# Weight loads ahead of the image, and two norms of the lone front by one matmul with Ln and Exp

## The chip, the cores and the metric

The kernel runs on one core of a Trainium2 chip. The core has a matrix engine (PE, its weight loads shown apart as PEld), a vector engine (DVE), an activation engine (ACT, ScalarE), a general one (POOL, GpSimd), a queue for transfers (SP, SyncE) and 16 DMA engines. Each works through its own list of instructions in order and waits for the others by semaphores. The metric is device time in microseconds, as the median of several runs. Beside it there is one profiled execution, from which the durations of single instructions are taken.

## What is computed

Two layers on a batch of 8 images of 64 channels and 128 x 128 pixels, all fp32. Layer 0 is a filter whose nine weights per pixel come from a small network. Layer 1 normalises the channels, runs a two-layer, two-direction state-space scan over the 16384 pixels, and follows with convolutions and a feed-forward part. What matters for this change:

```python
# layer 0
h = conv3x3(x, w1) + b1; h = where(h >= 0, h, 0.2 * h)       # 64 -> 32 channels
w_lp = softmax(conv1x1(h, w2) + b2)                          # 9 weights per pixel
x1 = x + sum_k x_shifted[k] * (delta[k] - w_lp[k])
# layer 1, its head: the front
def layernorm(v): c = v - mean(v); return c * rsqrt(mean(c * c) + 1e-5) * w + b   # over the 64 channels
x_norm = layernorm(x1)                                       # first norm
dw = conv1x1(x_norm, dw1) ...                                # a branch, used later
seq = layernorm(x_norm)                                      # second norm
hn = seq * rsqrt(mean(seq * seq) + 1e-5)                     # third norm, of the first scan layer
# then, twice: projections, a causal convolution, softplus, and in both directions
# h[t] = exp(dt[t] * A) * h[t-1] + dt[t] * B[t] * u[t];  y = sum over 16 states of h * C
```

## The kernel before

**Preparation.** The program begins with a block that loads the weights, turns them by small matmuls against an identity (`turned`, L206), and leaves them in the form that the matmuls need. It has two halves. The first makes the weights of the convolutions (`w1n` to `parts`, L227 to L303) in three staging tiles and stores those to DRAM (L305), from where each stage loads them later (`load_weights`, L492). The second half (L320 to L375) makes the weights of the scan, for two layers with two directions each: `wx`, `wz`, `wo`, `wbc`, `wdt`, `a_neg`, `dskip`. It loads `nw`, `inx`, `inz`, `on` once for each layer and `cw`, `xdt`, `xbc`, `dtn`, `al`, `dp` for each direction, each load standing beside its use; two bias vectors per direction (L371, L372) are loaded there too.

All transfers are issued by SyncE, in the order in which they are written (fills of the padding of the `hn` rows, L387 and L388, which stand outside the block, are put in between). So ahead of the second half's loads SyncE issues the first half's loads, the clearing of the padded image in DRAM (`clear(x_img)`, L89), the copying of image 0 into it in 16 pieces (`copy_x`, L98), the tap loads (L294) and the stores of the prepared weights (L305).

**The main part** is a list of small steps. Each `plan` writes its steps to a table under a time and a phase (`at`), and the table is emitted in sorted order, so each engine's list has the order of these times. Time 0 is the first scan unit, and a scan chunk of 1024 pixels takes 16 units.

**The front** (`Front`, L497) makes the head of layer 1 for 16 chunks of an image, each of two bands of four rows (128 partitions: 64 channels of each band, 512 pixels). Chunk c of image 0 is planned at a = -199 + 24 c. Chunks 0 to 7 have the flag `alone`, as they stand ahead of the scan (L651). Successive chunks overlap by design: while chunk c has its filter applied, chunk c+1 has its `hidden` convolution and `logits`, and chunk c-1 its norms. In the order of PE's list, one step of 24 time units holds, for neighbouring chunks: `centered` (L601), the means of the first norm (L469), three parts of `hidden` (L439, L444), the spread of the first norm (L484), `pointwise` (L618), `centered` again, the means of the second norm, its spread, the means of the third, the nine `weight` matmuls (L574) and the `logits` (L527, L528).

**A norm** (`Norm`, L463) has four steps. `means`: four matmuls whose stationary operand is a quarter of the squares and whose moving operand is `half_mean` (2 columns), which puts the means of 2 x 4 row pieces on pixels as partitions. `means_out`: ScalarE adds eps and brings 128 x 8 values to SBUF (L475). `root`: POOL raises them to the power -0.5 (L478). `spread`: eight matmuls that broadcast each value over 64 channels, into a PSUM tile `rb` (L484). DVE then multiplies by `rb` (L609). An fp32 matmul shows as two records in the profile.

The accumulators in PSUM are few: one bank `acc`, one `bg`, one `mm`, each with one buffer. `hidden` and `pointwise` both use `acc`, so `pointwise` waits until `hidden_out` (L520, L521) has read it. The scan (`Chunk`, L953) has ScalarE's `decay` (L1117), DVE's scan (L1135, L1137), POOL's `drive` (L1109), products on both (L1156, L1159), and activations SiLU (L1013) and Softplus (L1041), each with a table of its own on ScalarE.

Of the kernel before, what the change touches and what calls it, by code (L numbers as in the profile page):

```python
# [8 lines left out]
F32 = mybir.dt.float32  # L9
BF16 = mybir.dt.bfloat16  # L10
AF = mybir.ActivationFunctionType
# [4 lines left out]
P = 128  # L16
C = 64
# [5 lines left out]
DI = 128  # L23
DS = 16
DTR = 4
KC = 4
DEPTH = 2
# [28 lines left out]
def kernel(ctx: ExitStack, tc: tile.TileContext, a: dict, out: bass.AP):  # L56
# [6 lines left out]
    nc = tc.nc  # L63
# [3 lines left out]
    def row(v):  # L67
        return v.rearrange("(c o) -> c o", o=1)
# [3 lines left out]
    def const(shape, name, dt=F32):  # L72
        return wp.tile(shape, dt, tag=name, name=name)
# [3 lines left out]
    def dram(shape, name):  # L77
        return dramp.tile(shape, F32, tag=name, name=name + "_dram")


    def image(name):

        return dram([C, PW * PW + PW], name)

    def pixels(img):
        return img[:, 0 : PW * PW].rearrange("c (r w) -> c r w", w=PW)

    def clear(img, lo=0, hi=PW + 1):
        nc.sync.dma_start(  # L89
            img.rearrange("c (r w) -> c r w", w=PW)[:, lo:hi],  # L90
            zero.rearrange("c (o w) -> c o w", o=1).to_broadcast([C, hi - lo, PW]),
        )
# [6 lines left out]

    zero = const([C, PW], "zero")  # L100
    nc.vector.memset(zero, 0.0)
# [11 lines left out]
    eps = const([P, 1], "eps")  # L113
# [77 lines left out]
    with tc.tile_pool(name="wspill", bufs=1) as fp, tc.tile_pool(name="wprep", bufs=2) as pp, \  # L191
            tc.tile_pool(name="wps", bufs=4, space=PSUM) as pps:
        with tc.manual_schedule():
# [51 lines left out]
            for part in ((0, 0, 0, P), (1, 0, HID, P), (2, 0, HID + P, REST_HID), (2, C, P, REST_HID)):  # L245
                _, _, r0, n = part
                fn = pp.tile([P, C], F32, tag="fn", name="fn", bufs=4)
                nc.sync.dma_start(fn[0:n, :], fw[r0 : r0 + n, :])
                fdn = pp.tile([P, 9], F32, tag="fdn", name="fdn", bufs=4)
                nc.sync.dma_start(fdn[0:n, :], fd[r0 : r0 + n, :])  # L250
                parts.append((part, fn, fdn))
            clear(x_img)
            for i in range(NCH):
                copy_x(0, i)
# [63 lines left out]
                )  # L318

            for l in range(DEPTH):  # L320
                nw = pp.tile([P, 1], F32, tag="nw", name="nw")
                for h in range(2):
                    nc.sync.dma_start(nw[h * C : (h + 1) * C, :], row(a["L1_conv_m_norm_w"][l]))
                inx = pp.tile([DI, C], F32, tag="inx", name="inx")
                nc.sync.dma_start(inx, a["L1_conv_in_proj_w"][l, 0:DI, :])
                inz = pp.tile([DI, C], F32, tag="inz", name="inz")
                nc.sync.dma_start(inz, a["L1_conv_in_proj_w"][l, DI : 2 * DI, :])
# [3 lines left out]
                on = pp.tile([C, DI], F32, tag="on", name="on")  # L331
                nc.sync.dma_start(on, a["L1_conv_outproj_w"][l])
                for g in range(2):
                    to_blocks(
                        wo[:, l, g].rearrange("p i c -> p (i c)"),
                        turned(twice(on[:, C * g : C * g + C], C, C)[:, 0, :], ident[0:C, 0:C], P, C), C, C,
                    )
                for d in range(2):
                    cw = pp.tile([DI, KC], F32, tag="cw", name="cw")
                    nc.sync.dma_start(cw, a["L1_conv_conv_w"][l, d])  # L340
# [6 lines left out]
                    xdt = pp.tile([DTR, DI], F32, tag="xdt", name="xdt")  # L347
                    nc.sync.dma_start(xdt, a["L1_conv_xproj_w"][l, d, 0:DTR, :])
                    xbc = pp.tile([2 * DS, DI], F32, tag="xbc", name="xbc")
                    nc.sync.dma_start(xbc, a["L1_conv_xproj_w"][l, d, DTR : DTR + 2 * DS, :])  # L350
                    t = turned(xbc, ident[0:32, 0:32], DI, 32)
                    nc.scalar.copy(wbc[:, l, d, :], t[:, 0:32])
                    dtn = pp.tile([DI, DTR], F32, tag="dtn", name="dtn")
                    nc.sync.dma_start(dtn, a["L1_conv_dtproj_w"][l, d])
# [3 lines left out]
                    al = pp.tile([DI, DS], F32, tag="al", name="al")  # L358
                    nc.sync.dma_start(al, a["L1_conv_A_log"][l, d])
# [12 lines left out]
                    nc.sync.dma_start(dtb[:, l, d : d + 1], row(a["L1_conv_dtproj_b"][l, d]))  # L372
                    dp = pp.tile([DI, 1], F32, tag="dp", name="dp")
                    nc.sync.dma_start(dp, row(a["L1_conv_Dp"][l, d]))
                    nc.vector.tensor_scalar(dskip[:, l, d, :], ident, dp, None, ALU.mult)  # L375


# [18 lines left out]
    def at(time, phase, fn, *args):  # L396
        steps.setdefault((time, phase), []).append((fn, args))
# [65 lines left out]
    class Norm:  # L463


        def means(self, ps, sq):
            self.mp = ps("ms")
            for w in range(ROWS):
                nc.tensor.matmul(  # L469
                    self.mp[:, 2 * w : 2 * w + 2], sq[:, W * w : W * w + W], half_mean, start=True, stop=True  # L470
                )

        def means_out(self):
            self.r = wk.tile([P, 2 * ROWS], F32, tag="r", name="r", bufs=4)
            nc.scalar.activation(self.r, self.mp[:, 0 : 2 * ROWS], AF.Identity, bias=eps)  # L475

        def root(self):
            nc.gpsimd.tensor_tensor(self.r, self.r, neg_half, ALU.pow)  # L478

        def spread(self, ps):  # L480
            self.rb = ps("rb")
            for w in range(ROWS):
                for h in range(2):
                    nc.tensor.matmul(  # L484
                        self.rb[C * h : C * h + C, W * w : W * w + W],
                        self.r[:, 2 * w + h : 2 * w + h + 1].to_broadcast([P, C]), ident, start=True, stop=True,
                    )
# [9 lines left out]
    class Front:  # L497
# [860 lines left out]
```

## Time and profile before

| | |
|---|---|
| median of 3 runs | 29446.01 us (29431.68 to 29453.83) |
| the profiled execution | 29481.41 us, span 29479.5 us |
| granted PE clock, mean | 0.864 |
| busy share of the span | PE 79%, PEld 25%, DVE 93%, ACT 63%, POOL 94% |
| POOL's first `drive` | 505.0 us after the span's start |
| last of the preparation (`dskip`, L375) | 146.61 us |
| exponentials L539 of chunks 1 to 7 | 203.04, 243.68, 285.73, 326.54, 367.42, 408.34, 449.28 us |

The span runs from the first instruction to the last. Times of single instructions are microseconds from the span's start. A line of a timeline is one group of like instructions: start, length, engine, line of the source, operation, output and inputs, shapes, count, and in brackets how long the engine stood idle before it and what ended that.

### The profile page before, as it was taken

Reading aid. Unit: us, or ns where it says so; the run is one execution under the profiler, and the core shown is the slowest. Engines: PE = TensorE matmul, PEld = TensorE weight load, DVE = VectorE, ACT = ScalarE, POOL = GpSimd, SP = SyncE. Lnnn points to the kernel's source line nnn. Section 1 sums busy time; section 2 is a strip of 40 time slices with the busy share of each in tenths; the row PEclk is TensorE's granted clock in tenths of the full one; section 3 lists DMA queues with packets and bytes.
Section 4 is the critical chain, followed back from the end, with each engine's and each line's share of the span. In section 5 each row is a group of like instructions: output and inputs, shape, how many; then the busy total and the mean of one; then the engine's idle time right before and its main releaser. Section 6 shows DMA issues by size and latency. Waiting matters only on the chain. (4 is left out here: it accounts for less than half of the span.)

```text
span 29479.5 us, 312296 instructions
## 1 busy us (share of the span) xinstructions
PE 23358.6 (79%) x97708; PEld 7341.1 (25%) x97708; DVE 27316.3 (93%) x17567; ACT 18561.4 (63%) x28361; POOL 27648.1 (94%) x8732
## 2 busy tenths in 40 slices
PE   6666888878788787887878778787787877878678
PEld 3211222223222232222322223222222222222123
DVE  4999999999999999999999999999999999999997
ACT  3666666666666666666666666666666666666663
POOL 3999999999999999999999999999999999999994
PEclk7777888988889888988888888898888988889789
DMA  5776777767777678776787767777677776777674
GB/s 121 225 244 215 229 249 242 235 216 234 252 234 236 218 230 255 236 232 216 238 251 235 231 220 236 252 238 230 220 241 248 239 224 222 243 245 238 217 249 142
DMA packets 2592280, 6762.81 MB, mean 229 GB/s; under 512 B 431270, under 2 KB 736822, under 8 KB 2589462
## 3 DMA queue, kind: packets, MB, share of 16 engines
q1 hardware_dynamic: 2590614, 6742.83, 71.4%
q8 instruction: 773, 12.66, 0.2%
q14 instruction: 893, 7.32, 0.1%
HBM read 5509.49 MB, written 1265.19 MB: 230 GB/s over the span
## 5 line engine op out<-in xcount | busy, mean ns | idle before, releaser
L1109 POOL TENSOR_TENSOR bu<-dup,bp 128x2048 f32<-128x2048 f32 x4096 | 18564.5, 4537 | 370.7 <-DVE w L1137 238.3
L1117 ACT ACTIVATE w<-dtp,a_neg 128x1024 f32<-128x1024 f32 x8192 | 9159.6, 1118 | 800.4 <-DVE hs L1135 341.3
L1156 POOL TENSOR_TENSOR hs<-hs,cp 128x1024 f32<-128x1024 f32 x2832 | 6678.4, 2358 | 250.2 <-ACT state L1149 191.9
L1159 DVE TENSOR_TENSOR hs<-w,cp 128x1024 f32<-128x1024 f32 x5360 | 6562.7, 1224 | 361.7 <-DMA cp<-bc_dram 132.8
L1137 DVE TENSOR_TENSOR_SCAN w<-w,state,bu 128x1024 f32<-128x1024 f32 x2683 | 6290.4, 2345 | 292.8 <-ACT w L1117 291.9
L1135 DVE TENSOR_TENSOR_SCAN w<-w,state,bu 128x1024 f32<-128x1024 f32 x2677 | 6278.7, 2345 | 243.6 <-ACT w L1117 241.3
L1175 PE MATMUL y<-hs,sel_y 128*32 128x512 f32 x32768 | 5121.8, 700 | 60.6 <-POOL hs L1156 60.3
L1149 ACT COPY state<-w 128x1 f32<-128x1 f32 x5360 | 837.9, 156 | 5524.7 <-DVE hs L1159 5474.4
L1137 DVE TENSOR_TENSOR_SCAN hs<-w,state,bu 128x1024 f32<-128x1024 f32 x1413 | 3308.2, 2341 | 209.9 <-issue 121.7
L1135 DVE TENSOR_TENSOR_SCAN hs<-w,state,bu 128x1024 f32<-128x1024 f32 x1419 | 3321.0, 2340 | 41.3 <-ACT state L1149 16.7
L1168 PE MATMUL y<-xc,dskip 128*64 128x512 f32 x4096 | 1577.5, 860 | 1660.6 <-ACT yv L1192 1392.1
L987 PE MATMUL xp<-hn,wx 128*128 128x512 f32 x4096 | 2350.5, 703 | 669.3 <-ACT xc L993 469.2
L819 PE MATMUL fp<-fw,bgw 128*128 128x512 f32 (+1 forms) x5760 | 2270.0, 637 | 104.6 <-ACT ga L866 71.7
L1149 ACT COPY state<-hs 128x1 f32<-128x1 f32 x2832 | 541.4, 191 | 1968.6 <-DVE hs L1137 1018.6
L1175 PEld LDWEIGHTS y<-hs,sel_y 128*32 128x32 f32 x32768 | 729.8, 117 | 3676.1 <-issue 2444.1
L1028 PE MATMUL dp<-xc,wdt 128*128 128x512 f32 x2048 | 1237.5, 688 | 462.1 <-ACT dt L1035 362.6
L478 POOL TENSOR_TENSOR r<-r,neg_half 128x8 f32<-128x8 f32 x768 | 1262.6, 1644 | 300.7 <-ACT r L475 279.2
L1117 ACT ACT_TABLE_LOAD x1134 | 1454.9, 1283 | 20.0
L1065 POOL TENSOR_TENSOR dt<-dt,xc 128x1024 f32<-128x1024 f32 x512 | 1211.2, 2366 | 221.8 <-DMA dt_dram<-dt 187.7
L825 PE MATMUL fp<-fw,bgw 64*128 64x512 f32 (+1 forms) x5760 | 1415.3, 610 | 0.0
L589 PE MATMUL acc<-t,ident 128*128 128x512 f32 x2160 | 1265.5, 669 | 85.6 <-DVE hc L609 84.7
L987 PEld LDWEIGHTS xp<-hn,wx 128*128 128x128 f32 x4096 | 830.8, 216 | 1988.2 <-issue 964.3
(214 smaller groups left out, 25747.8 us busy)
## 6 DMA issues: line engine op xcount, KB each, us to landing
bp<-bc_dram SPq DMA_DIRECT2D x4096, 256.0 KB, 4.2
dup<-du_dram SPq DMA_DIRECT2D x4096, 256.0 KB, 5.0
dtp<-dt_dram SPq DMA_DIRECT2D x4096, 256.0 KB, 5.0
cp<-bc_dram SPq DMA_DIRECT2D x4096, 256.0 KB, 5.0
hn<-hn_dram SPq DMA_DIRECT2D x1024, 256.5 KB, 4.9
dt_dram<-dt SPq DMA_DIRECT2D x512, 512.0 KB, 3.4
du_dram<-dt SPq DMA_DIRECT2D x512, 512.0 KB, 2.6
yf_dram<-yv SPq DMA_DIRECT2D x512, 256.0 KB, 4.7
```

The source lines that it names most:

```text
L819: nc.tensor.matmul(o, wpair[:, i, g, m], self.win[h][:, i : i + ROWS, 0:W], start=(i == 0), stop=False)
L825: nc.tensor.matmul(o, wlast[rows, i, g, m], self.win[h][rows, i : i + ROWS, lo : W + lo], start=False, stop=(i == 2),)
L987: nc.tensor.matmul(self.xp[h], wx[:, self.l, self.d, i, :], self.hn2[:, s.start + 2 * i : s.stop + 2 * i], start=(i == 0), stop=(i == 1),)
L1109: nc.gpsimd.tensor_tensor(bu, self.dup[self.pairs[k][1]], self.over_pair("bp", k), ALU.mult)
L1117: nc.scalar.activation(w, self.dtp[gp][:, i, :], AF.Exp, scale=a_neg[:, self.l, self.d, g, j : j + 1])
L1135: nc.vector.tensor_tensor_scan(to, w, bu, s0, ALU.mult, ALU.add)
L1137: nc.vector.tensor_tensor_scan(to[:, ::-1], w[:, ::-1], bu[:, ::-1], s0, ALU.mult, ALU.add)
L1149: nc.scalar.copy(self.column(u), h[:, T - 1 : T] if self.d == 0 else h[:, 0:1])
L1156: nc.gpsimd.tensor_tensor(hs, hs, c, ALU.mult)
L1159: nc.vector.tensor_tensor(hs, w, c, ALU.mult)
L1168: nc.tensor.matmul(self.y[C * h : C * h + C, :], dskip[:, self.l, self.d, C * gp : C * gp + C], self.xc[:, s], start=True, stop=False,)
L1175: nc.tensor.matmul(self.y[lo : lo + 32, :], sel_y, hs[:, i, s], start=False, stop=(k % 4 == 3))
```

## The change

It has two parts.

*Loads.* The 34 loads of the second half of the preparation (`nw` to `dp`, all but the bias vectors) are issued in a loop of their own ahead of `clear(x_img)` and `copy_x`. Their tiles get as many buffers as there are layers, or layers and directions, and are looked up in the dictionary `own` where they are used. What is computed from them, and where, stays.

*Norms.* For chunks with `alone`, norms `n1` and `n2` (not `n3`) use one matmul with a 128 x 128 constant `mean_c`, which has 1/64 in its two diagonal blocks, so that the mean over the 64 channels arrives on every channel. ScalarE takes the logarithm of mean plus eps in place in PSUM, then the exponential of -0.5 times that. `root` and `spread` do nothing for these. Ahead of the list of steps, ScalarE is told to load a table set that holds both functions.

```diff
+EXP_AND_LN = "natural_log_exp_and_others"
...
+    mean_c = const([P, P], "mean_c")
+    nc.vector.memset(mean_c, 0.0)
+    nc.vector.memset(mean_c[0:C, 0:C], 1.0 / C)
+    nc.vector.memset(mean_c[C:P, C:P], 1.0 / C)
...
+            own = {}
+            for l in range(DEPTH):
+                nw = pp.tile([P, 1], F32, tag="nw", name="nw", bufs=2)
+                for h in range(2):
+                    nc.sync.dma_start(nw[h * C : (h + 1) * C, :], row(a["L1_conv_m_norm_w"][l]))
+                own[l, "nw"] = nw
+                inx = pp.tile([DI, C], F32, tag="inx", name="inx", bufs=2)
+                nc.sync.dma_start(inx, a["L1_conv_in_proj_w"][l, 0:DI, :])
+                own[l, "inx"] = inx
...
+                for d in range(2):
+                    cw = pp.tile([DI, KC], F32, tag="cw", name="cw", bufs=4)
+                    nc.sync.dma_start(cw, a["L1_conv_conv_w"][l, d])
+                    own[l, d, "cw"] = cw
...
             clear(x_img)
             for i in range(NCH):
                 copy_x(0, i)
...
-                inx = pp.tile([DI, C], F32, tag="inx", name="inx")
-                nc.sync.dma_start(inx, a["L1_conv_in_proj_w"][l, 0:DI, :])
...
+                inx = own[l, "inx"]
...
     class Norm:
+        alone = False
+
         def means(self, ps, sq):
+            if self.alone:
+                self.rb = ps("rb")
+                nc.tensor.matmul(self.rb, mean_c, sq, start=True, stop=True)
+                return
             self.mp = ps("ms")
...
         def means_out(self):
+            if self.alone:
+                nc.scalar.activation(self.rb, self.rb, AF.Ln, bias=eps)
+                nc.scalar.activation(self.rb, self.rb, AF.Exp, scale=-0.5)
+                return
...
         def root(self):
+            if self.alone:
+                return
...
         def spread(self, ps):
+            if self.alone:
+                return
...
-            self.alone = a + FRONT_STEP < -2
+            self.alone = n1.alone = n2.alone = a + FRONT_STEP < -2
...
     with tc.manual_schedule():
+        nc.scalar.preload_act_table_set(EXP_AND_LN)
         for key in sorted(steps):
```

More of the change, by code (lines that the diff above doesn't have):

```diff
@@ L251 @@
                 parts.append((part, fn, fdn))
+            own = {}
[7 more added lines that the diff above has]
+                own[l, "inx"] = inx
+                inz = pp.tile([DI, C], F32, tag="inz", name="inz", bufs=2)
+                nc.sync.dma_start(inz, a["L1_conv_in_proj_w"][l, DI : 2 * DI, :])
+                own[l, "inz"] = inz
+                on = pp.tile([C, DI], F32, tag="on", name="on", bufs=2)
+                nc.sync.dma_start(on, a["L1_conv_outproj_w"][l])
+                own[l, "on"] = on
+                for d in range(2):
+                    cw = pp.tile([DI, KC], F32, tag="cw", name="cw", bufs=4)
+                    nc.sync.dma_start(cw, a["L1_conv_conv_w"][l, d])
+                    own[l, d, "cw"] = cw
+                    xdt = pp.tile([DTR, DI], F32, tag="xdt", name="xdt", bufs=4)
+                    nc.sync.dma_start(xdt, a["L1_conv_xproj_w"][l, d, 0:DTR, :])
+                    own[l, d, "xdt"] = xdt
+                    xbc = pp.tile([2 * DS, DI], F32, tag="xbc", name="xbc", bufs=4)
+                    nc.sync.dma_start(xbc, a["L1_conv_xproj_w"][l, d, DTR : DTR + 2 * DS, :])
+                    own[l, d, "xbc"] = xbc
+                    dtn = pp.tile([DI, DTR], F32, tag="dtn", name="dtn", bufs=4)
+                    nc.sync.dma_start(dtn, a["L1_conv_dtproj_w"][l, d])
+                    own[l, d, "dtn"] = dtn
+                    al = pp.tile([DI, DS], F32, tag="al", name="al", bufs=4)
+                    nc.sync.dma_start(al, a["L1_conv_A_log"][l, d])
+                    own[l, d, "al"] = al
+                    dp = pp.tile([DI, 1], F32, tag="dp", name="dp", bufs=4)
+                    nc.sync.dma_start(dp, row(a["L1_conv_Dp"][l, d]))
+                    own[l, d, "dp"] = dp
             clear(x_img)
@@ L320 @@
             for l in range(DEPTH):
-                nw = pp.tile([P, 1], F32, tag="nw", name="nw")
-                for h in range(2):
-                    nc.sync.dma_start(nw[h * C : (h + 1) * C, :], row(a["L1_conv_m_norm_w"][l]))
-                inx = pp.tile([DI, C], F32, tag="inx", name="inx")
-                nc.sync.dma_start(inx, a["L1_conv_in_proj_w"][l, 0:DI, :])
-                inz = pp.tile([DI, C], F32, tag="inz", name="inz")
-                nc.sync.dma_start(inz, a["L1_conv_in_proj_w"][l, DI : 2 * DI, :])
+                nw = own[l, "nw"]
+                inx = own[l, "inx"]
+                inz = own[l, "inz"]
                 inx2 = twice(inx, DI, C)[:, 0, :]
@@ L330 @@
                 nc.vector.tensor_scalar(wz[:, l, :], t[:, 0:DI], nw, None, ALU.mult)
-                on = pp.tile([C, DI], F32, tag="on", name="on")
-                nc.sync.dma_start(on, a["L1_conv_outproj_w"][l])
+                on = own[l, "on"]
                 for g in range(2):
@@ L338 @@
                 for d in range(2):
-                    cw = pp.tile([DI, KC], F32, tag="cw", name="cw")
-                    nc.sync.dma_start(cw, a["L1_conv_conv_w"][l, d])
+                    cw = own[l, d, "cw"]
                     taps = by_taps(inx2, cw, DI, KC)
@@ L346 @@
                         nc.vector.tensor_scalar(wx[lo, l, d, at // 2, :], t[lo, 0:DI], nw[lo], None, ALU.mult)
[L347 to L350, printed above, removed]
+                    xdt = own[l, d, "xdt"]
+                    xbc = own[l, d, "xbc"]
                     t = turned(xbc, ident[0:32, 0:32], DI, 32)
                     nc.scalar.copy(wbc[:, l, d, :], t[:, 0:32])
[L353 to L354 removed]
+                    dtn = own[l, d, "dtn"]
                     dtt = pp.tile([DTR, DI], F32, tag="dtt", name="dtt")
@@ L357 @@
                     nc.scalar.copy(wdt[:, l, d, :], turned(xdt, dtt, DI, DI)[:, 0:DI])
-                    al = pp.tile([DI, DS], F32, tag="al", name="al")
-                    nc.sync.dma_start(al, a["L1_conv_A_log"][l, d])
+                    al = own[l, d, "al"]
                     nc.scalar.activation(al, al, AF.Exp)
@@ L372 @@
                     nc.sync.dma_start(dtb[:, l, d : d + 1], row(a["L1_conv_dtproj_b"][l, d]))
-                    dp = pp.tile([DI, 1], F32, tag="dp", name="dp")
-                    nc.sync.dma_start(dp, row(a["L1_conv_Dp"][l, d]))
+                    dp = own[l, d, "dp"]
                     nc.vector.tensor_scalar(dskip[:, l, d, :], ident, dp, None, ALU.mult)
```

## The prediction

> **What bounds the kernel now.** I read the page first: its slices are level at 9 tenths on DVE and POOL from the second slice on, and lower in the first. The change touches the weight preparation and the front of image 0 only, so the first slice is what counts. Next I read windows of 50 us over the first 600 us.
>
> ```profile
> 50.00:100.00 50.00, 4.04 (x18) 3.91 (x18) 3.31 (x13) 0.58 (x3) 0.00 (x0) 0.50 1.14 104
> 300.00:350.00 50.00, 35.60 (x148) 18.98 (x148) 14.04 (x25) 11.94 (x25) 6.35 (x7) 0.66 0.19 51
> 550.00:600.00 50.00, 42.08 (x187) 13.07 (x186) 48.58 (x36) 31.08 (x49) 48.64 (x17) 0.86 0.63 207
> ```
>
> The columns are the window, its length, then PE, PEld, DVE, ACT, POOL busy, granted clock, DMA share, GB/s. There are three regimes: at 50 us only the DMAs work; at 300 us the front runs alone and no engine is full, so a chain of dependent steps sets the pace; from about 505 us the scan fills POOL, then DVE. Time lost ahead of the scan is added to the end one for one, as every engine works its list in the written order. Then the waits of the first 520 us, and SyncE's own waits:
>
> ```profile
> ACT twice L203 <- DMA inx<-in_L_conv_in_proj_w: 51.1, 1, 51.1
> SPq L431 <- DVE dskip L375: 18.2, 1, 18.2
> ```
>
> The second half of the preparation (the scan's weights) waits 51.1 us for its first load; then the first window load (L431) waits 18.2 us for the last instruction of that preparation, whose SBUF it takes over. The timeline of SyncE's queue shows why:
>
> ```profile
> 22.88 0.59 SPq L89 DMA_DIRECT2D x_dram<-zero  x1
> 88.27 4.68 SPq L294 DMA_DIRECT2D w<-in_L_conv_ffn_dw_w  x4
> 100.77 0.32 SPq L305 DMA_DIRECT2D w_dram<-w  x1
> 103.52 0.73 SPq L325 DMA_DIRECT2D inx<-in_L_conv_in_proj_w  x1
> 147.03 2.38 SPq L431 DMA_DIRECT2D xa<-x_dram  x4
> ```
>
> The image is cleared (issued at 22.88) and copied (the queue shows the sixteen copies from 55.38 to 88.27), and inx stands behind both. Preparation then runs from 106.5 to 146.9, that is 40.4 us. Last, the timeline of one front step, 40.88 us from one L539 (326.54) to the next (367.42):
>
> ```profile
> 332.54 1.64 POOL L478 TENSOR_TENSOR r<-r,neg_half 128x8 f32<-128x8 f32 x1 [2.26 <-ACT r L475]
> 337.97 1.09 PE L484 MATMUL rb<-ident,r 128*64 128x128 f32 x16
> 342.07 1.12 PE L618 MATMUL dwp<-hc,bgw 128*128 128x512 f32 x2 [3.00 <-ACT ha L521]
> 343.97 2.08 PE L601 MATMUL cp<-hc,center 128*128 128x512 f32 x2 [0.78 <-ACT dwt L622]
> 347.21 1.87 PE L469 MATMUL ms<-half_mean,sq 128*128 128x2 f32 x8 [0.61 <-ACT hc L606]
> 349.46 1.64 POOL L478 TENSOR_TENSOR r<-r,neg_half 128x8 f32<-128x8 f32 x1 [14.33 <-ACT r L475]
> 351.15 1.98 PE L484 MATMUL rb<-ident,r 128*64 128x128 f32 x16 [1.62 <-POOL r L478]
> 353.24 0.69 DVE L609 TENSOR_TENSOR hc<-hc,rb 128x512 f32<-128x512 f32 x1 [2.99 <-PE rb L484]
> ```
>
> The first norm's spread (337.97) stands on PE behind the hidden convolution; the second norm is a bare chain from 347.21 to 353.24.
>
> [...] mean granted clock is 0.66 in the front, and L601 takes 2.08 us here but 1.13 at 471.75. [...] L622 (bias) 687 ns, L605 (square) 597 ns. [...] here a load takes 1283 and the next activation follows at once (475.42, then 476.71).
>
> **The change, part by part.**
>
> *A. Loads moved.* 34 DMAs of the scan's weights (nw two per layer, inx, inz, on, and six per direction) leave the place behind L305 and go ahead of the image clear. In that place layer 0 took 11.5 us (101.14 to 112.68), 1.9 of it for the four bias loads that stay; layer 1's unblocked issues come to about 7.5. I take 16 us of SyncE (15 to 17). So clear, copies, wtap loads and weight stores all come 16 us later: the clear at 38.9, the last store at 116.8. What still stands before the first window load is eight bias loads of 0.47 (3.8) and a zero fill (0.5): about 121.5 in place of 147.03. Preparation, its weights landed by about 41, starts at 56.2, ends near 97, and is hidden behind the image with 24 us to spare. What is late next is the image, on SyncE's queue. Gain 25.5; I take 25. If that cover were gone (image late by 25), A would be nothing. The clear of dw_img (DMA share over 1 from 150 to 190) and the first xb wait on it simply shift along.
>
> *B. Norms one and two, chunks 0 to 7 (n3 keeps its old form).* Per norm, out go 8 small matmuls, one 0.27 Identity, one POOL power (1.64), 16 spread matmuls; in come one 128x128x512 fp32 matmul (2 records, priced by L601), Ln (0.69) and Exp (0.60).
>
> n1: the mean matmul takes the place of L469's 1.05 at full clock, so hidden starts as before (332.08). Ln, Exp, the L609 multiply and L613 end near 335.1, all under hidden, which ends at 337.97. ScalarE's hidden_out needs only PE: start 338.1, so L618 at 339.4 in place of 342.07: 2.67 less.
>
> n2: at half clock, 2.11 (L601's start to L605's) + 0.73 + 0.65 = 3.49 from start to L609, in place of 6.03: 2.54 less. After L609 the step is as before: DVE's multiplies and PE's logits are unchanged.
>
> That is 5.21 for each of the six steps from 203.0 to 449.3: 31.3.
>
> *Clock.* With dwp 2.7 us nearer to hidden, the idle stretch that now drops the clock at 343.7 mostly disappears; [...] I estimate that 4 steps in 5 keep full clock through L601 and the mean (0.9 us each, from 2.08 against 1.13), less 0.25 for a later warm-up now and then: 1.2 a step, 7.2 in all. The bounds are -5 (hidden caught cold for a window, each step) and +11. I take +5.
>
> *Chunk 6* (449 to 502) has chunk 0's first convolution and SiLU between. Hidden_out then waits for L993, so n1 gives 1.0; the convolution that ran at half clock (467.04, 3.36 us against 1.98) may give 1.4; Ln and Exp put SiLU's table load back by 1.1. Between 0 and 5; I take 2.5.
>
> *Chunk 7* runs with the scan's start: POOL loses two powers (3.3 us) while full, but the tables of SiLU, Softplus and Exp alternate, so Ln and Exp need 2 to 4 extra loads of 1.28, some of them ahead of a decay that has 2.3 us of slack. Between -3 and +4; I take 1.
>
> *Costed at nothing:* the preload of the table (1.28, ScalarE idle from 144 to 162 before and waiting for the image after), three memsets on DVE at 2 us (about 0.1 to 0.2 each, L109 to L111; DVE idles 8.3 us before w1n lands), more SBUF.
>
> Sum: 25 + 31.3 + 5 + 2.5 + 1 = 65 us. The profiled execution took 29481.41 us with a span of 29479.5, so 2 us lie around it, outside the change; its steps are priced in that execution, and I take the sum from the median, which stands 35 us below it: 29446 - 65 = 29381.
>
> **The rivals.**
> 1. *The image is later than I count* (more descriptors in flight, window loads waiting for the 1.3 MB store): A falls to 12, total 52, 29394. For: DMA share is over 1.2 while it moves. Against: stores landed in 4 to 6 us.
> 2. *Ln and Exp do not share a table*, so every norm pays two loads: n2's 2.54 is eaten by 2.57, n1's stays hidden, and the clock gains nothing; 25 + 16 + 1 = 42, 29404. Against: the preload names the set.
> 3. *Hidden falls to half clock*: 11.3 us in place of 5.9, B gives nothing, 25 remains, 29421. Against: cp and the mean keep PE busy ahead of it.
> 4. *Slower: the scan itself is changed for good.* The new constant and the pools move SBUF addresses; 512 scan chunks of some 56.6 us each (28,970 us behind the start) outweigh the start if each takes over 65/512 = 0.127 us more. At 0.25 it gives 29446 - 65 + 128 = 29509. For: POOL and DVE are over 90% busy together. Against: L1109 stays between 4484 and 4660 ns over all its buffers, and the order is the same.
>
> **How the numbers follow.** Forecast 0.70, with its own range 29368 to 29398; rivals 0.12, 0.07, 0.05, 0.06. Range 29360 to 29415: it takes in rivals 1 and 2 and the forecast's unknowns, and leaves out 3 and 4. A measurement of this kernel can't tell less than 0.2% from no change, that is 59 us, 29387. The forecast lies just past it: three quarters of its chance (0.53) with a little of rival 1 fall beyond, together 0.55; within 0.40 (the rest of the forecast, rivals 1 to 3); slower 0.05 (rival 4).
>
> **What would show it.** A: no 51 us wait on inx; first L431 near 121.5 and not released by dskip. B: six steps of about 35 us between L539s in place of 41; L618 right behind L521; no L478 for n1 and n2 before 500 us. Clock: L601 at 1.1 behind L618. Scan rows unchanged to the nanosecond or so. The prediction is wrong if L431 comes after 130, if table loads appear between the steps, or if L1109, L1137, L1159 have other means.

## The result

The kernel after takes 29376.54 us (median of 15 executions, 29346.33 to 29416.47), the kernel before on the same chip 29439.03 (29417.36 to 29453.83): 62.5 us less, a ratio of 0.9981 with a 95% interval of 0.9974 to 0.9988. The profiled execution of after took 29416.47 us, with a span of 29414.7. Both profiled executions are long ones: that of before (29481.41 us) lies above its 15 timed ones, that of after is the longest of its 15.

The windows of the kernel after at the three places shown for the one before (columns: window, length, busy time of PE, PEld, DVE, ACT, POOL, granted clock, DMA share, GB/s):

```profile
50.00:100.00 50.00, 31.46 (x118) 25.48 (x118) 20.04 (x83) 6.26 (x31) 0.00 (x0) 0.50 1.14 122
300.00:350.00 50.00, 39.19 (x131) 18.71 (x132) 19.80 (x37) 13.57 (x28) 3.41 (x7) 0.64 0.23 64
550.00:600.00 50.00, 41.93 (x171) 15.01 (x167) 46.45 (x37) 27.92 (x44) 48.13 (x16) 0.81 0.59 196
```

At 50 us PE now works (31.46 us, before 4.04) while the DMAs carry the image: that is the second half of the preparation. At 300 us the front still runs alone, a little denser. The scan's window looks as before. SyncE's queue in the timeline of the kernel after:

```profile
23.98 0.59 SPq L265 DMA_DIRECT2D inx<-in_L_conv_in_proj_w  x1
39.31 0.59 SPq L91 DMA_DIRECT2D x_dram<-zero  x1
69.04 29.95 SPq L100 DMA_DIRECT2D x_dram<-in_x  x16
99.09 3.83 SPq L334 DMA_DIRECT2D w<-in_L_conv_ffn_dw_w  x4
111.14 0.32 SPq L345 DMA_DIRECT2D w_dram<-w  x1
117.31 2.40 SPq L460 DMA_DIRECT2D xa<-x_dram  x4
```

inx goes out at 23.98 instead of 103.52, and its wait of 51.1 us is gone. The clear goes out 16.4 us later (39.31 against 22.88). The last instruction of the preparation (`dskip`, now L404) is done at 96.5, 21 us ahead of the first window load, which comes at 117.31 instead of 147.03. So it is now the image, and the stores behind it, that hold up the first window load. One front step of the kernel after, 33.57 us from the exponential at 272.38 to the next at 305.95:

```profile
276.72 1.12 PE L500 MATMUL rb<-sq,mean_c 128*128 128x512 f32 x2 [0.69 <-ACT sq L648]
282.68 1.05 PE L473 MATMUL hp<-xa,bgw 64*32 64x512 f32 x4
285.11 1.12 PE L661 MATMUL dwp<-hc,bgw 128*128 128x512 f32 x2 [1.38 <-ACT ha L564]
287.01 1.12 PE L644 MATMUL cp<-hc,center 128*128 128x512 f32 x2 [0.78 <-ACT dwt L665]
289.30 1.12 PE L500 MATMUL rb<-sq,mean_c 128*128 128x512 f32 x2 [0.83 <-ACT hc L649]
290.47 0.66 ACT L510 ACTIVATE rb<-rb,eps 128x512 f32<-128x512 f32 x1 [0.75 <-PE rb L500]
291.16 0.58 ACT L511 ACTIVATE rb<-rb 128x512 f32<-128x512 f32 x1
291.78 0.69 DVE L652 TENSOR_TENSOR hc<-hc,rb 128x512 f32<-128x512 f32 x1 [0.40 <-ACT rb L511]
```

Nothing stands between hidden's last matmul (282.68) and dwp (285.11) but `hidden_out`. The second norm goes from the start of cp (287.01) to its multiply (291.78) in 4.77 us; before it took 9.27 (343.97 to 353.24). And cp and the mean behind it run at full clock, 1.12 each, where cp took 2.08 before.

The instructions of the scan take as long as before: drive 4539 ns in the mean (before 4537), the larger group of scans 2345 (2345), DVE's product 1225 (1224).

To follow the 73.4 us by which the first scan starts earlier (440.79 against 514.23), each front step can be cut at four points that all kernels have: the exponential of the softmax, dwp (the output of `pointwise`), the second cp (the output of the second `centered`) and the issue of the next window load (xa). The first norm lies in the first stretch, the second in the third. The table gives the mean over the six steps between the exponentials of chunks 1 and 7, in us, with the time of the first window load and the start of the first scan.

| kernel | first xa | exponential to dwp (n1) | dwp to 2nd cp | 2nd cp to xa issue (n2) | to the next exponential | step | first scan |
|---|---|---|---|---|---|---|---|
| before | 147.03 | 15.57 | 2.06 | 11.16 | 12.24 | 41.04 | 514.23 |
| after | 117.31 | 13.31 | 1.90 | 7.23 | 12.25 | 34.70 | 440.79 |
| loads alone | 120.62 | 15.72 | 2.06 | 11.21 | 12.25 | 41.24 | 486.06 |
| norms alone | 143.98 | 13.42 | 1.90 | 7.30 | 12.24 | 34.86 | 473.86 |
| n1 alone, with loads | 122.04 | 13.67 | 1.90 | 9.76 | 12.24 | 37.58 | 464.99 |
| n2 alone, with loads | 121.52 | 17.10 | 1.90 | 8.59 | 12.26 | 39.85 | 480.61 |
| no preload | 120.57 | 14.49 | 1.90 | 8.54 | 12.24 | 37.18 | 468.42 |
| dummy matmuls | 121.61 | 14.45 | 1.90 | 6.70 | 13.99 | 37.04 | 469.58 |
| chunk 7 in the old form | 121.34 | 13.22 | 1.90 | 7.09 | 12.25 | 34.46 | 445.24 |
| the same, and n3 | 116.39 | 12.61 | 1.90 | 7.23 | 12.43 | 34.17 | 436.13 |
| n3, chunk 7 new | 116.78 | 12.51 | 1.90 | 7.12 | 12.45 | 33.98 | 435.18 |
| after, again | 125.76 | 13.44 | 1.90 | 7.15 | 12.26 | 34.76 | 452.97 |

The two stretches that hold no norm keep their length to 0.2 us, apart from the kernel with dummies. All that the change does in a step is in the two stretches named n1 and n2.

### The profile page after: what moved, and what is told of

Read it like the earlier page. It is cut to its first block, busy times and chain, and to the rows that moved or that the text cites. A ratio compares the mean times of both kernels' runs of the same rounds, so it can differ in the third digit from the quotient of the medians.

```text
span 29414.7 us, 311582 instructions
## 1 busy us (share of the span) xinstructions
PE 23404.7 (80%) x97356; PEld 7317.8 (25%) x97356; DVE 27321.0 (93%) x17570; ACT 18581.3 (63%) x28381; POOL 27624.7 (94%) x8716
## 5 line engine op out<-in xcount | busy, mean ns | idle before, releaser
L1152 POOL TENSOR_TENSOR bu<-dup,bp 128x2048 f32<-128x2048 f32 x4096 | 18571.6, 4539 | 369.3 <-DVE w L1180 236.3
L1202 DVE TENSOR_TENSOR hs<-w,cp 128x1024 f32<-128x1024 f32 x5360 | 6563.9, 1225 | 322.5 <-DMA cp<-bc_dram 91.5
L1180 DVE TENSOR_TENSOR_SCAN w<-w,state,bu 128x1024 f32<-128x1024 f32 x2683 | 6292.2, 2345 | 297.7 <-ACT w L1160 296.7
L1180 DVE TENSOR_TENSOR_SCAN hs<-w,state,bu 128x1024 f32<-128x1024 f32 x1413 | 3308.6, 2342 | 227.5 <-issue 121.5
```

The source lines that it names most:

```text
L1152: nc.gpsimd.tensor_tensor(bu, self.dup[self.pairs[k][1]], self.over_pair("bp", k), ALU.mult)
L1180: nc.vector.tensor_tensor_scan(to[:, ::-1], w[:, ::-1], bu[:, ::-1], s0, ALU.mult, ALU.add)
L1202: nc.vector.tensor_tensor(hs, w, c, ALU.mult)
```

## Experiments

**Each part alone.** Loads alone: the kernel after with the old norms and without the preload.

```diff
-            self.alone = n1.alone = n2.alone = a + FRONT_STEP < -2
+            self.alone = a + FRONT_STEP < -2
...
-        nc.scalar.preload_act_table_set(EXP_AND_LN)
```

> The moved loads alone, with the old norms. Theory (the parts add up, each only shifts what stands behind it): first window load at 117 us in place of 147, first L539-like exponential near 136.5 (30 less), chunk 0's step some 3 us shorter as in the changed kernel, every later front step 41 us as before, POOL's first drive near 472 (33 less than 505.0); time 27 to 37 us less. Rival (the parts share their gain, the earlier image being worth little without the shorter steps): drive less than 20 us earlier, time within 20 of before.

Norms alone: the kernel before with the new `Norm`, its constant, its flags and the preload; the loads stay behind the image.

> The new norms alone, with the loads where they were. Theory: first window load at 147.0 as before; six front steps of 33.5 to 35 us in place of 41, drive near 466 (38 to 40 less than 505.0), chunk 0 of the scan 1 to 3 us longer for the table loads of chunk 7; time 30 to 42 us less. Rival (it is the clock's phase, which the moved loads set): steps of 36 to 38, the second centered matmul at 2.1 us in some of them.

Loads alone took 29431.51 us against 29452.1 for before, a ratio of 0.9994 (0.9985 to 1.0002): 20.6 us, which the interval does not tell from nothing. In its trace the first window load is 26.4 us earlier, the scan 28.2, and the steps are those of before. That is less than was expected (33 at the first drive, 27 to 37 at the end), but the rival's sign, a drive less than 20 us earlier, did not come. Norms alone took 29422.47, a ratio of 0.9990 (0.9983 to 0.9996), 29.6 us less; so a tenth of a per cent could be told from nothing here, half of what the prediction allowed for. Its steps are 34.86 in the mean, with one of six second cps at half clock, and the scan starts 40.4 us earlier, though its first load is only 3.0 earlier. At the start of the scan the parts add up to 28.2 + 40.4 = 68.6, and both together gave 73.4. Of the 4.8 between them, 3.1 is chunk 6's step, 55.79 with the norms alone and 52.73 in the kernel after: in it n1's stretch is 2.6 us longer, with hidden at half clock.

**Each norm alone.**

```diff
-            self.alone = n1.alone = n2.alone = a + FRONT_STEP < -2
+            self.alone = n1.alone = a + FRONT_STEP < -2
```

> The changed kernel with only the first norm in the new form for the lone chunks. Theory (the first norm's gain is 2.67 us a step, and it is what brings the pointwise matmul close enough to the hidden convolution for the clock to stay full, so the clock's gain comes with it): second centered matmul at 0.70 us a record in most steps, steps of 36.5 to 37.5 us. Rival (the two are independent, the clock's gain comes with the denser mean matmuls): records at 1.22, steps of 38.2.

and with `n2.alone` in the place of `n1.alone`:

> The changed kernel with only the second norm in the new form. Theory: the second centered matmul stays at half clock (1.22 us a record) in all or nearly all steps, as the idle stretch after the hidden convolution is as long as before; steps of 38.2 to 38.6 us (40.9 less 2.54). Rival: records at 0.70 and steps of 36.5 to 37.5.

In one execution each they took 29411.74 and 29438.92 us, with 29454.09 for before. n1 alone shortens its own stretch by 1.90, and also that of n2, which it does not touch, by 1.40: dwp follows hidden sooner, and the second cp (1.12 in all six steps) keeps the full clock. n2 alone shortens its own stretch by 2.57, at half clock throughout, and n1's becomes 1.53 longer. A timeline of one such step shows where:

```profile
217.55 1.86 PE L504 MATMUL ms<-half_mean,sq 128*128 128x2 f32 x8 [0.69 <-ACT sq L648]
219.34 1.92 PE L468 MATMUL hp<-xa,bgw 128*32 128x512 f32 x4
221.19 1.67 PE L473 MATMUL hp<-xa,bgw 64*32 64x512 f32 x4
```

The mean of n1 takes 1.86 (before 1.05 at 248.46), hidden's first two groups 1.92 and 1.67 (before 1.05 each). The windows of the same trace, PE alone (window, length, PE busy, granted clock, DMA share, GB/s), show the clock rise:

```profile
215.65:219.07 3.42, 2.73 (x10) 0.50 0.56 135
219.07:222.48 3.41, 3.41 (x10) 0.50 0.23 63
222.48:225.89 3.41, 3.41 (x16) 1.00 0.00 0
```

The full clock comes at 222.48, 9.7 us behind the exponential; in the step of before that starts at 243.68 it comes at 248.14, 4.5 us behind. So the 2.57 gained on n2 is nearly all paid back in n1's stretch in four steps of six (40.7 to 40.8 each; the other two 37.9 and 38.1). The expectation had cp right, at half clock, and the steps wrong in these four (38.2 to 38.6). For n1 alone it held nearly, with 37.58 for 36.5 to 37.5. The two singles give 3.46 + 1.19 = 4.65 a step, both together 6.34. The difference lies in n1's stretch, which the pair shortens by 2.26 and the singles, added up, by 0.37, and there it is hidden's clock.

**The table set.** The preload is taken away.

```diff
-        nc.scalar.preload_act_table_set(EXP_AND_LN)
```

> The changed kernel without the preload of the table set. Theory (Ln and Exp sit in one set only because it is loaded by name): two table loads of 1.28 in each of the 14 norms of chunks 0 to 6, those of the first norm hidden under the convolution, those of the second on the path: steps of about 37.3 in place of 34.7, drive 15 to 18 us later than in the changed kernel. Rival (the set is chosen so without being told, or the loads are hidden): steps of 34.7, drive at 432.

29432.42 us in one execution. ScalarE's list in the timeline of one second norm:

```profile
303.87 1.28 ACT L510 ACT_TABLE_LOAD   x1
305.17 0.66 ACT L510 ACTIVATE rb<-rb,eps 128x512 f32<-128x512 f32 x1
305.85 1.28 ACT L511 ACT_TABLE_LOAD   x1
307.14 0.58 ACT L511 ACTIVATE rb<-rb 128x512 f32<-128x512 f32 x1
```

Without the preload a load of 1.28 us stands ahead of the logarithm (303.87) and another ahead of the exponential (305.85), and so in each of these norms: 48 loads in the first 600 us in place of 20. A step is 2.48 longer than in the kernel after, 1.31 of it in n2's stretch and 1.18 in n1's, where the mean and hidden's first group meet the half clock (2.08 and 1.84 in the step from 284.34). The scan starts 27.6 us later: 3.3 of that is the first window load, 14.9 the six steps, and 8.0 chunk 6's step (60.73 against 52.73), where two groups of the scan's first convolution also run at half clock (3.48 and 3.78 instead of 1.88 and 1.98). The expectation had the steps right (37.3; measured 37.18) and the first drive too early (15 to 18 us later; measured 27.1). In the kernel after no load stands between the preload (0.72) and SiLU's (402.27), while 14 norms take their logarithm and their exponential in between; no row of before had shown that the named set serves both. It takes the explicit load to get this here.

**Where the loads stand.** The moved loads go behind the clear instead of ahead of it, still ahead of the copies.

```diff
+            clear(x_img)
             own = {}
             for l in range(DEPTH):
...
-            clear(x_img)
             for i in range(NCH):
                 copy_x(0, i)
```

> The changed kernel with the clearing of the image issued ahead of the moved loads, so that SyncE issues these while the clearing runs. Theory (the image's chain sets the front's start, and 16 us of SyncE's issuing stand in it, of which part would be hidden behind the clearing): first window load at 108 to 114 us in place of 117 to 121. Rival (the transfers are full from the clearing on, so it makes no difference where the issue time is, or the loads then stand behind the clearing's descriptors and the preparation becomes the wait): 117 or later.

The rival held; 29440.64 us in one execution, with 29454.09 for before. SyncE's queue in the timeline of this kernel:

```profile
22.90 0.59 SPq L91 DMA_DIRECT2D x_dram<-zero  x1
23.53 24.54 SPq L263 DMA_DIRECT2D nw<-in_L_conv_m_norm_w  x2
...
66.34 31.42 SPq L100 DMA_DIRECT2D x_dram<-in_x  x16
...
120.39 2.39 SPq L460 DMA_DIRECT2D xa<-x_dram  x4
```

The two small loads right behind the clear take 24.54 us to issue. In the kernel after it is a fill of `hn_dram` that stands there and takes 23.13 (39.95 to 63.08). In the kernel before, the same fill takes 24.18 (23.51 to 47.69). So the queue stood still for 23 to 25 us behind the clear with the fill next as with the loads next, and the issues of the loads are not hidden in it: the copies start at 66.34 instead of 69.04. Those 2.7 us are given back by four fills of `hn_dram`, which stood behind the clear and are now issued right ahead of the first window load (117.72 to 120.2). The first window load comes at 120.39, and the place ahead of the clear is as good as this one.

**Chunk 7.** Chunks 0 to 6 in the new form, chunk 7, whose norms run beside the first scan chunk, in the old.

```diff
-            self.alone = n1.alone = n2.alone = a + FRONT_STEP < -2
+            self.alone = a + FRONT_STEP < -2
+            n1.alone = n2.alone = self.alone and self.c < 7
```

> The changed kernel with the new norms for chunks 0 to 6 only, chunk 7 keeping the old ones, so that the four table loads at the scan's start are gone and two powers are back on POOL. Theory (those loads cost what chunk 0 of the scan lost): first scan 1 to 2 us sooner behind the first drive than the 8.4 of the changed kernel or the same, chunk 0 near 59.7 in place of 61.1. Rival (the loss is the transfers' issue on SyncE, which the tables do not touch): chunk 0 stays at 61 or more, with DVE's wait for cp of about 2.4 us still there.

29408.06 us in one execution. In the kernel after, the timeline of ScalarE shows what chunk 7 pays:

```profile
431.76 1.28 ACT L510 ACT_TABLE_LOAD   x1
...
433.74 1.28 ACT L511 ACT_TABLE_LOAD   x1
```

and the same pair again at 459.79 and 461.76. The preload helps here only until another set is loaded (SiLU's at 402.27): behind it Ln and Exp of chunk 7 pay one load of 1.28 us each, four in all, as in the kernel without the preload (459.39 and 461.36, 486.47 and 488.45 there). Without the four loads the first scan chunk lasts 57.70 us, with them 61.11; before it lasted 59.70. So the expectation (59.7) had the cause right for this one chunk. By chunk 12 no gain can be seen: from the last exponential ahead of the scan to the first scan of chunk 12 it is 699.2 us here and 699.7 in the kernel after, but 695.8 in the repeat of the kernel after below and 695.4 before.

**A clock held up on purpose.** If clock is what is lost, a busier PE might keep it: two dummy matmuls beside each of the `weight` matmuls and one beside each piece of the logits, into a PSUM tile that nobody reads.

```diff
+    def warm(n):
+        y = py.tile([P, N], F32, tag="y", name="warm")
+        for _ in range(n):
+            nc.tensor.matmul(y, identb[0:65, :], wts[0], start=True, stop=True)
...
                 nc.tensor.matmul(o, self.ha[0:64, W * r : W * r + W], w2a, start=False, stop=True)
+                if self.alone and 0 < self.c:
+                    warm(1)
...
             nc.tensor.matmul(self.wb, sel_k[:, k].rearrange("k h c -> k (h c)"), self.wt, start=True, stop=True)
+            if self.alone and self.c < 7:
+                warm(2)
```

> The changed kernel with idle matmuls added in the lone front (two bf16 ones of 512 columns behind each filter-weight matmul, one behind each row of the logits), whose output nobody reads, to keep PE's activity up in the half step that runs at half clock. Theory (clock is what is left in the step): logits, third norm's spread and first centered matmul run at full clock, steps 31.5 to 33.5 us in place of 34.7, drive 8 to 20 us sooner. Rival (the added matmuls cost PE what the clock gives, or the clock does not respond to them): steps of 34.5 to 36.

The rival's mechanism held, at steps of 35.0 to 37.5, mostly above its range of 34.5 to 36; 29431.12 us in one execution. The timeline of PE, and one window of it:

```profile
275.97 0.60 PE L495 MATMUL warm<-wt,identb 65*128 65x512 bf16 x2
...
276.79 1.06 PE L495 MATMUL warm<-wt,identb 65*128 65x512 bf16 x2
...
279.84:283.25 3.41, 3.41 (x10) 0.50 0.00 0
...
290.55 2.08 PE L653 MATMUL cp<-t,center 128*128 128x512 f32 x2
```

The clock falls in the midst of the dummies (a pair takes 0.60, then 1.06) and stays low to the next cp, although PE has no gap worth naming from 276.40 to 288. The dummies cost 1.74 us between xa and the next exponential; n2's stretch is now 6.70 in every step, but n1's is 14.45.

Which windows at half clock are followed by full clock can be counted in all 14 profiles of this case together. Between 200 and 400 us their granted clock changes only on a grid of 3.41 us. There they hold 512 windows of this grid at half clock, and 78 of them are followed by full clock. If the logits (fp32 with 18 columns) and all bf16 matmuls (the dummies and the `weight` matmuls among them) are left out, the remaining matmuls leave PE idle for at most 0.45 us in each of the 78, and for at least 0.49 us in each of the other 434. (The ends of matmuls are modelled in a profile, so the border is no exact figure.) If all matmuls are counted there is no such border: 48 windows without idle time, 18 of them in this kernel, are not followed by full clock. Why there is a border only without these matmuls, for their type or for their shape, no run held apart. n2 alone agrees with it: the window from 215.65 above is idle for 0.69 us and half clock goes on, the next is filled and full clock follows. So does the one step of the kernel after that meets hidden at half clock: the window from 272.05 is idle for 0.44 us and the clock rises, the one from 340.32 for 0.51 us and it does not.

**The third norm too.** Chunks 0 to 5 take n3 by the same matmul; chunk 7 stays in the old form.

```diff
-            self.alone = n1.alone = n2.alone = a + FRONT_STEP < -2
+            self.alone = a + FRONT_STEP < -2
+            n1.alone = n2.alone = self.alone and self.c < 7
...
-            at(a + 38, REST, lambda: n3.means(bg_tile, self.sq))
+            n3.alone = self.alone and self.c < 6
+            at(a + 38, REST, lambda: n3.means(mm_tile if n3.alone else bg_tile, self.sq))
```

> Chunks 0 to 6 take n1 and n2 by one matmul, chunks 0 to 5 also n3; the rest takes the power, and everything else is as in the kernel after. Theory (what a norm costs on this path is its spread matmul and its way through the power, so n3 gives up its spread ahead of the first cp as well): no L527 behind the exponential, the first cp starts at the exponential instead of 2.02 us behind it, steps of 31.5 to 33.5 us in place of 33.6 to 37.1, first drive at 188 to 199 (208.17 in the kernel after), chunk 0 near 57.7 instead of 61.1, median 9 to 18 us under the kernel after, 29359 to 29368 on the chip and beside the before of the kernel after, ratio to before 0.9975 or less. Rival 1 (the clock takes it back: with less work ahead of the first cp the full clock comes later in the step, as with n2 alone, where n1's stretch grew from 13.5 to 16.0): steps stay at 34.5 to 36, first drive at 204 to 209, ratio 0.998. Rival 2 (a gain at the front no longer reaches the end): the first drive comes early, yet the ratio stays at 0.998 or above.

The expectation has a slip: 208.17 is the sum of the six steps of the kernel after, not the time of its first drive (432.38), and "188 to 199" was meant for that sum. Measured: the sum is 205.03, the first drive 426.92, the median 29375.05 us against 29415.26 for before on that chip, a ratio of 0.9983 (0.9976 to 0.9990). The mechanism of rival 1 held, at steps of 33.4 to 34.5, a little below its range. The spread is gone and cp starts beside the exponential, but the timeline shows what it meets:

```profile
269.38 2.07 PE L644 MATMUL cp<-t,center 128*128 128x512 f32 x2
272.14 2.07 PE L500 MATMUL rb<-sq,mean_c 128*128 128x512 f32 x2 [0.69 <-ACT sq L648]
274.14 1.92 PE L468 MATMUL hp<-xa,bgw 128*32 128x512 f32 x4
275.99 1.38 PE L473 MATMUL hp<-xa,bgw 64*32 64x512 f32 x4
```

cp, mean and hidden's first two groups run at half clock, 2.07, 2.07, 1.92 and 1.38, where the kernel after had 1.64, 1.12, 1.05 and 1.05 in the step from 272.38. In the kernel after the spread of n3 and cp fill the window from 272.05 but for 0.44 us, and the clock rises 3.1 us behind the exponential. Without the spread the window with cp and the mean is idle for 0.69 us, and the clock rises 6.6 us behind. Of the 2.02 us taken out ahead of cp, 0.61 is left in n1's stretch (13.22 to 12.61), and n3's mean gives 0.18 of that back (12.25 to 12.43). It doesn't measurably beat the kernel after. Rival 2 is not ruled out either: the drive came 5.5 us earlier than in the kernel after, yet the ratio stayed above 0.998.

> As the kernel after (n1 and n2 in the new form for chunks 0 to 7), with n3 also in that form for chunks 0 to 5. Beside the run of the kernel with chunk 7 left in the old form it tells whether n3 and chunk 7 add up. Theory: steps as in that run, 31.5 to 33.5; chunk 0 stays near 61.1, since chunk 7's norms still pay four loads of tables beside the scan; so 2 to 4 us more than the other run. Rival (the clock takes it back): steps 34.5 to 36.

With chunk 7 in the new form as well: steps of 33.3 to 34.6, three of them at the lower end of the rival's range (34.5 to 36) and three at the upper end of the theory's (31.5 to 33.5), the first scan chunk 60.49, and 29323.88 us in its one execution, 91 us below before. It was run again, with the kernel after beside it on one chip.

> The kernel after, unchanged, beside the kernel with n3 in the new form and beside runs of before on the same chip. Theory (the front's gain, 68 to 73 us at the start of the scan, reaches the end whole): 60 to 73 us below before, ratio 0.9975 to 0.998. Rival (the scan gives a part back): 30 to 50 us below, ratio 0.9983 to 0.999, as the run of the six chunks with n3 had it (0.9983, 40 us).

> n1 and n2 in the new form for chunks 0 to 7, n3 for chunks 0 to 5, timed. In its one look it took 29323.88, 91 us below before, though its scan started only 5.6 us ahead of the kernel after and chunk 12 9 us ahead. Theory (that look caught the good end of a wander which the scan has in any kernel): median 3 to 12 us below the kernel after on the same chip, the profile at the start of the scan again near 435. Rival (with this front the scan falls into a better pattern for good): 25 to 60 us below the kernel after.

The kernel after took 29424.63 us (29403.68 to 29461.08), 51.7 below the 29476.37 of before there, a ratio of 0.9982 (0.9973 to 0.9991), between the two expectations and near its first value of 0.9981. The one with n3 took 29422.25, 54.1 below, a ratio of 0.9981 (0.9972 to 0.9991): 2.4 us below the kernel after, so the 91 us of one execution did not come again, and the theory's 3 to 12 us were just missed. Its scan started at 447.91 and not near 435: the first window load came 8.2 us later than in the run before (124.96), and the step from chunk 0's exponential to chunk 1's took 4.3 us more.

## Why the prediction was right

It said 29381 us from a gain of 65. Measured were 62.5 and, on another chip, 51.7, both with intervals that hold 65 (some 35 to 77 and 27 to 80 us). At the start of the scan, where the terms can be told apart, the gain is 73.4 and 61.3 in the two profiles of the kernel after. The mechanism was right in its main parts. That the median came within 2.5 us of the sum is in part luck: in the profile the terms miss by up to 5 us each, up and down, and a part of the gain at the start is not found in the medians.

*A, 25 us: right.* The first window load is 29.7 us earlier in one profile and 21.3 in the other; in all profiles with moved loads it stands between 116.39 and 125.76, with a median of 121.0, against the 121.5 worked out. What moves it is when the copies of the image can start behind the clear (69.04 in the first profile, 72.22 in the second) and how long they take (29.95 and 35.19). The cover of 24 us for the preparation was 21 (96.5 to 117.31). Rival 1 (the image is late) fell.

*B, n1 2.67: right where hidden is at full clock.* In five of the six steps n1's stretch is 12.7 to 13.0, 2.5 to 2.9 shorter; in the sixth (340.71) hidden's first groups are at half clock and it is 15.57, as before. The mean is 2.26.

*B, n2 2.54: right.* Alone and at half clock it measured 2.57.

*Clock, 5 us over six steps: about right, and larger than its term.* In all, the six steps gave 246.25 - 208.17 = 38.1 us against 31.3 + 5 = 36.3. n2's stretch is 3.93 shorter, 1.36 more than n2 alone, since cp is at full clock in all six steps and the mean wholly in two of them (6.70; 7.4 to 7.6 otherwise). n1's stretch loses 0.4 of its 2.67 to a later rise. Both movements that the prediction weighed are in the trace. In the kernel before, PE is busy for 1.12 us of the window from 340.30 to 343.70, at a granted clock of 1.00, and the clock is 0.50 from 343.70 to 347.10; that is the fall that was expected to go. In the six steps of the kernel after the full clock lasts 10.24, 13.65 or 17.07 us, multiples of the 3.41 us of the grid above. So a step's length decides in which window of the grid the next one meets its matmuls. The four steps in five were the author's estimate. A window in which PE is merely busy was not enough for full clock, as the 48 windows without idle time counted above show.

*A term left out.* The step from chunk 0's exponential to chunk 1's was not in the six. It went from 36.42 to 33.10: 3.3 us. In the repeat it was 0.7, in loads alone 2.4 and in norms alone 1.2, so little of it is sure. The stretch from the first window load to the first exponential gave 0.4 more.

*Chunk 6, 2.5: too much.* Its step went from 53.19 to 52.73, and from the last exponential to the drive 2.55 became 1.86: 1.2 in all. Which of its three pieces was too large is not shown.

*Chunk 7, 1: not told from nothing.* Four table loads, as priced, and the first scan chunk 1.4 us longer than before (0.6 in the repeat). Up to chunk 12 the old form and the new differ by 0.5 us, and two profiles of the kernel after by 3.9, so that the sign is open.

So the sum at the start of the scan is 29.7 + 0.4 + 3.3 + 38.1 + 1.2 = 72.7, and with 0.8 between drive and scan, rounded, 73.4. It dips to 62.7 at the scan's chunk 7. At chunk 12 the gain is 67.6 and stays so within 0.4 us to chunk 32; in the repeat it is 60.1. From there on it moves in every kernel, mostly by 10 to 40 us, with means of drive and of the scans within 0.2% of those of before; in loads alone it goes from 24.6 to 55.4 by the end, and in the execution that took 29323.88 us from 77.3 to 157.4. The end of one profile therefore says little about a change of this size; the medians do. No run held apart what sets this movement.

The prediction also has time lost ahead of the scan reach the end one for one. That is not shown: in all six comparisons of medians the gain is smaller than at chunk 12 of the profile (62.5 for 67.6, 51.7 for 60.1, 20.6 for 24.6 with loads alone, 29.6 for 37.8 with norms alone, 40.2 for 73.8 and 54.1 for 64.7 with n3). All profiles are set against a single one of before, so whether these microseconds get lost in the scan or that profile was a late one stays open.

*Rivals.* 2 (two loads a norm) was the real danger: it is what the kernel does without its preload (48 loads against 20). It costs 2.5 us a step, but n2's stretch stays 2.6 us shorter than before, since cp keeps the full clock. 3 (hidden at half clock) came in one step of six, and in n2 alone, in four. 4 (the scan changed for good) did not come, as the gain keeps still over 20 scan chunks.

## To carry to other kernels

A stretch in which one chain of dependent steps sets the pace is priced by adding up what is taken off that chain; but where PE is half idle, the clock must be priced with it, as the place of each matmul in the step decides whether it takes 1.12 or 2.08 us. Removing one piece of work can take the clock away from another: n2 alone gained 2.57 and gave 1.53 back, n3 took out 2.0 us of matmuls, the clock rose 6.6 us behind the exponential instead of 3.1, and 0.6 was kept, while n1 and n2 together gained 6.34 a step, where each by itself gave 3.46 and 1.19. And when loads wait behind a large transfer, ask what that leaves at the head of the queue: here the preparation was freed by 51 us and the front could start only 21 to 30 us sooner, as the image became the next to be late.

## What was not expected of the hardware

- Dummy bf16 matmuls and logits without a gap from 276.40 to 288 did not raise the clock (1.06 a pair of dummies against 0.60 at full clock; granted clock 0.50 from 279.84 to 283.25). In 512 windows of 3.41 us at half clock, full clock followed the 78 in which the other fp32 matmuls left at most 0.45 us idle, and none of the 434 in which they left 0.49 or more.
- Behind the clear of the image the next issue took SyncE 24.18 us in the kernel before and 23.13 in the kernel after, where it was a fill of `hn_dram`, and 24.54 where it was two small loads.
- A table load of 1.28 us is followed at once by its activation (303.87, then 305.17), and part of it hides in the wait for the matmul (the mean's runs from 303.44 for 1.13 us, the load from 303.87): a pair of loads lengthened n2's stretch by 1.31 to 1.84 us, not by 2.57.
